# An empty place between the choice of experts and its counts, in a mixture of experts that runs between attention matmuls

## The chip, the cores and the metric

The kernel runs on one core of one Trainium2 chip. The metric is the device time of one execution in microseconds (us); the time before is the median of 3 runs. All data is fp32. A core has five engines that matter here, each with its own queue of instructions that it works off in order: TensorE (PE in the profile, its weight loads PEld), VectorE (DVE), ScalarE (ACT), GpSimd (POOL) and SyncE (SP, which here starts plain DMA transfers). Instructions wait for other engines through semaphores.

## The reference: what is computed

Four layers on x of 4 blocks by 512 tokens by 128 features. Each layer adds half a feed-forward part, an attention, and half a feed-forward part again, each after a layernorm:

```
x = x + 0.5 * ffn(layernorm(x));  x = x + attn(layernorm(x));  x = x + 0.5 * ffn(layernorm(x))
```

The change is in layer 2's feed-forward part, a mixture of 8 experts in which each token goes to one expert, and an expert takes at most 64 tokens of a block (n: 512 tokens, e: 8 experts, c: 64 slots):

```
gates = softmax(x @ Wg);  expert_idx = argmax(gates);  mask = one_hot(expert_idx)
gate = sum(gates * mask)
pos = cumsum(mask, axis=tokens) * mask - mask          # place in the expert's queue
keep = mask * (pos < 64)
dispatch = keep[..., None] * one_hot(pos, 64);  combine = dispatch * gate
expert_inputs  = einsum('bnd,bnec->becd', x, dispatch)
h              = gelu(einsum('becd,edh->bech', expert_inputs, W1))     # 512 hidden
expert_outputs = einsum('bech,ehd->becd', h, W2)
out            = einsum('becd,bnec->bnd', expert_outputs, combine)
```

Layer 2's attention is causal with 16 heads of 8, layer 3's the same without the mask. Layer 3's feed-forward part works on channels (a receptance gate, a squared ReLU, and a shift by one token).

## The kernel before, in words

**Where the time of interest lies.** Layer 2's attention of blocks 0 to 3 and layer 3's attention of blocks 0 to 3 are run as one list of 8 rows (`padded_attn_quick`). A row is worked off in 8 rounds. A round computes scores (L1462, PE, into `big`, a PSUM tile of 128 x 1024 of which there are three), the exponential (L1465, ACT, `pT`, six tiles), for causal rows a mask on the diagonal (L1469, DVE), and the values of the round before (L1475, PE, into `one`, a PSUM tile of 128 x 512 of which there are two). At the end of a row stand the sums by head (L1481, PE), a reciprocal (L1483, DVE), its spreading over the features (L1490, PE; L1492, DVE) and the output projection (L1497, PE; L326, DVE). At a row's beginning stand a layernorm, transposes (L315, PE), the products for values (L1435) and for keys and queries (L1444).

**What is put between.** Other work is written as Python generators whose pieces are fetched by `side` at three places of each round: A (L1599, ahead of the values), B (L1619, behind them) and C (L1622, behind the second half of the scores; `whole` is false there). `side` fetches up to three pieces at A and B and two at C. A piece tells by what it yields what the next one is: PE says that the next piece begins with matmuls, and then it is not begun at C; LATER says the same and also ends the place; WAIT only ends the place. A plan lists the streams with the first and the last row they may be in; `before(k)` works off what is due by row k. Layer 2 has four mixtures on two blocks each (two half layers, two pairs of blocks); the first half layer of blocks 0 and 1 is done by other code, and the other three (`l2_pair`) are in that plan. The first mixture (rounds 0 to 10) is the first half layer of blocks 2 and 3, the second (rounds 18 to 28) the second half layer of blocks 0 and 1, the third (rounds 34 to 44) the second half layer of blocks 2 and 3. After the second and the third, layer 3's channel streams follow in the plan (layernorm L295 on POOL, L304 on DVE; transposes L315; L1888, L1889 on DVE; L1894 on PE).

**The pieces of one mixture**, in the program's order: two layernorms; transposes and the router's products (L1640); softmax, the shares and the ranks of the experts (DVE); the choice `m` of the first expert (L1788, the trace calls it `chosen`) with its running sums (L1651, L1653) and the gates (L1644, L1645); then, after a LATER, the counts of tokens ahead of each token (L1658, L1659, PE), and the slots made of them (L1664 to L1675, L1798, L1799, DVE, `islot`); two empty places; eight scatters of normalised tokens into `pair_x` in HBM, two a piece (L1805, indirect DMAs on POOL); one load of all experts' inputs X, 512 KB (L1813, SP); three empty places; transposes of X (L1822, PE, one `big`) and their copy (L1823, DVE); four products with W1, each in a `big` of its own (L1830), copied to `hr` (L1832, DVE, 1.2 us each); gelu on the four (L1837, ACT, about 1.06 us each, another table of functions than the exponential's, so that a table load of 1.28 us stands at each change); two products with W2 (L1844), copied (L1846) and stored to HBM (L1847, SP, 256 KB each); two empty places; eight gathers by token (L1861, indirect DMAs on POOL, `yg`, four tiles), each token's result added to x with its gate (L1856, DVE, kept in the program's order).

**What sets the final order.** The generators and `side` set the order in which instructions are handed to the tile framework; its scheduler then sets each engine's own order by priorities and dependencies, so that an instruction can come out earlier or later than it was handed in. Some orders are fixed by hand: the adds L1856, the layernorm's outputs, and that the load of X waits for all eight scatters.

In the trace of before the first mixture's counts start at 906 us, its scatters run from 912.2 to 922.4, X's transposes start at 927.4 and the gathers at 960.1. In the second mixture the scatters start at 1045.5, X's transposes at 1064.7, the gathers at 1093.2; in the third the counts start at 1181.2, the scatters at 1188.0, the gathers at 1237.3.

Of the kernel before, what the change touches and what calls it, by code (L numbers as in the profile page):

```python
# [243 lines left out]
def program(ctx: ExitStack, tc: tile.TileContext, a: dict, out: bass.AP, worst):  # L244
# [12 lines left out]
    def one():  # L257
        return ps.tile([P, 512], F32, tag="one", name="one", bufs=2)
# [1372 lines left out]
    PE, LATER, WAIT = "PE", "PE later", "wait"  # L1631
# [10 lines left out]
    def l2_gates(sh, m, n, gt):  # L1642
        pick = tiny.tile([P, n, NE], F32, tag="pick", name="pick", bufs=1)
        nc.vector.scalar_tensor_tensor(pick, sh, 0.5, m, ALU.mult, ALU.mult)  # L1644
        nc.vector.tensor_reduce(gt, pick, AX.X, ALU.add)  # L1645

    def l2_sofar(m, n):

        v = m.rearrange("p (i t) e -> p i t e", i=n)
        sofar = tiny.tile([P, n, NT - 1, NE], F32, tag="sofar2", name="sofar2", bufs=1)  # L1650
        nc.vector.tensor_copy(sofar[:, :, 0, :], v[:, :, 0, :])  # L1651
        for t in range(1, NT - 1):
            nc.vector.tensor_tensor(sofar[:, :, t, :], sofar[:, :, t - 1, :], v[:, :, t, :], ALU.add)  # L1653
        return sofar
# [99 lines left out]
    def l2_pair(w, work, rows, rooms, key):  # L1754
# [33 lines left out]
        nc.vector.tensor_scalar(m, rank, 1.0, None, ALU.is_lt)  # L1788
        sofar = l2_sofar(m, 2)
        l2_gates(sh, m, n, gates)  # L1790
        yield LATER
        pp = one()
        before = pp[:, : n * NE].rearrange("p (t e) -> p t e", t=n)
# [236 lines left out]
    with tc.tile_pool(name="w13", bufs=1, reuse_waits="tile") as wp:  # L2030
# [50 lines left out]
        else:  # L2081
            deep[0] = 3
            rows = [(n, b, causal) for n, causal in (("l2", True), ("l3", False)) for b in range(B)]
            with tc.tile_pool(name="work", bufs=1, reuse_waits="tile") as work:

                def mixture(i, key):
                    return l2_pair(w2, work, (2 * i, 2 * i + 1), pair_rooms[i], key)
# [48 lines left out]
```

## Time and profile before

| what | before |
|---|---|
| median of 3 runs | 1448.82 us (1446.33 to 1449.94) |
| profiled execution | 1449.85 us |
| its span, first to last instruction | 1448.1 us |
| mean granted TensorE clock | 0.929 of full speed |
| PE busy | 1265.3 us, 87% of the span |
| DVE busy | 964.2 us, 67% |
| ACT busy | 647.2 us, 45% |
| POOL busy | 289.3 us, 20% |
| wait of L1658 for `chosen`, first two paired mixtures | 5.0 us, 2 waits |
| the same, third mixture | 0.7 us, 1 wait |

All times in the profile come from one execution, the profiled one, and start at its first instruction. The rows used below come from a few views. A row of the timeline gives start, length, engine, line, operation, output and inputs with their shapes, the number of instructions in the group, and in square brackets the idle time ahead of it with what ended it. [...] A row of the view of waits gives the waiting line, the engine and line that it waited for, and the total, the number and the longest of these waits. A row of the view of windows gives a stretch of the span, its length, the busy time of each engine with the number of its instructions, then the granted clock of TensorE (1.00 is full speed), the share of the DMA engines and GB/s.

### The profile page before, as it was taken

Reading aid. Unit: us, or ns where it says so; the run is one execution under the profiler, and the core shown is the slowest. Engines: PE = TensorE matmul, PEld = TensorE weight load, DVE = VectorE, ACT = ScalarE, POOL = GpSimd, SP = SyncE. Lnnn points to the kernel's source line nnn. Section 1 sums busy time; section 2 is a strip of 40 time slices with the busy share of each in tenths; the row PEclk is TensorE's granted clock in tenths of the full one; section 3 lists DMA queues with packets and bytes.
Section 4 is the critical chain, followed back from the end, with each engine's and each line's share of the span. In section 5 each row is a group of like instructions: output and inputs, shape, how many; then the busy total and the mean of one; then the engine's idle time right before and its main releaser. Section 6 shows DMA issues by size and latency. Waiting matters only on the chain.

```text
span 1448.1 us, 19903 instructions
## 1 busy us (share of the span) xinstructions
PE 1265.3 (87%) x6894; PEld 657.8 (45%) x6894; DVE 964.2 (67%) x2395; ACT 647.2 (45%) x925; POOL 289.3 (20%) x279
## 2 busy tenths in 40 slices
PE   6899899999899999899875597889887899899995
PEld 3455453344253435455544484453454345433333
DVE  4796677989888885967776547466655744365324
ACT  2435346636445362345543243335343446445560
POOL 3420420322103020202344113220112120210000
PEclk9999899999999999999987698799899989989996
DMA  7123121111111020122114000010001000100000
GB/s 274 38 72 107 49 70 61 66 52 53 69 45 73 30 71 8 37 59 61 30 46 170 0 1 1 30 30 1 6 25 30 1 8 23 29 1 12 4 8 11
DMA packets 60097, 63.78 MB, mean 44 GB/s; under 512 B 11089, under 2 KB 51282, under 8 KB 59346
## 3 DMA queue, kind: packets, MB, share of 16 engines
q1 hardware_dynamic: 54354, 50.86, 10.3%
q0 software_dynamic: 5632, 11.55, 2.6%
q8 instruction: 58, 0.95, 0.3%
q14 instruction: 53, 0.43, 0.1%
HBM read 28.95 MB, written 16.65 MB: 31 GB/s over the span
## 4 chain that ended last, share of the span: by engine, by line
PE 58%; DVE 20%; issue 11%; ACT 4%; POOL 3%; DMA 1%; SPq 1%; another core or an unknown queue 1%; POOLq 0%; DVEq 0%; ACTq 0%
PE big L1462 7%; PE big L734 7%; PE one L1475 6%; PE big L1043 5%; PE one L1057 5%; ACT pT L1465 2%; PE big L993 2%; PE one L767 2%; PE one L1497 2%; PE one L1086 2%; DVE sums L1052 2%; PE one L315 1%; PE big L1830 1%; PE one L1844 1%; PE big L1444 1%
## 5 line engine op out<-in xcount | busy, mean ns | idle before, releaser
L1465 ACT ACTIVATE pT<-big 128x1024 f32<-128x1024 f32 (+3 forms) x256 | 205.3, 866 | 235.1 <-PE big L1462 213.8
L1462 PE MATMUL big<-qkq,qkk 32*128 32x512 f32 (+3 forms) x1024 | 180.9, 581 | 30.7 <-ACT pT L1465 19.6
L734 PE MATMUL big<-w_w,xsT 128*128 x312 | 151.8, 610 | 0.4 <-issue 0.3
L1044 ACT ACTIVATE pT<-big 128x1024 f32<-128x1024 f32 x128 | 125.8, 1035 | 55.0 <-PE big L1043 52.4
L295 POOL TENSOR_TENSOR rs<-rs,root 128x4 f32<-128x4 f32 x51 | 56.8, 1116 | 422.9 <-DVE rs L294 368.2
L1043 PE MATMUL big<-qk 64*128 64x512 f32 x512 | 126.6, 605 | 6.8 <-DVE U L1079 6.8
L1475 PE MATMUL one<-pT,V 128*32 128x512 f32 (+3 forms) x1024 | 124.0, 570 | 1.3 <-DVE pT L1469 0.9
L1462 PEld LDWEIGHTS big<-qkq,qkk 32*128 32x128 f32 x1024 | 65.5, 193 | 119.7 <-ACT pT L1465 49.3
L815 POOL DMA_INDIRECT yg<-sorted_y,ito x64 | 72.1, 1126 | 225.6 <-DMA sorted_y<-ys 78.2
L1057 PE MATMUL one<-pT,V 128*64 128x512 f32 x512 | 116.9, 598 | 0.0
L559 POOL DMA_INDIRECT sorted_x<-xn,irows x64 | 70.5, 1102 | 70.3 <-DVE share L531 22.4
L1052 DVE TENSOR_TENSOR sums<-sums,pT 128x1024 f32<-128x1024 f32 x64 | 78.1, 1220 | 5.1 <-ACT qk L995 0.5
L1043 PEld LDWEIGHTS big<-qk 64*128 64x128 f32 x512 | 46.3, 186 | 69.0 <-issue 40.6
L1469 DVE TENSOR_TENSOR pT<-pT,w_c_tri 128x256 f32<-128x256 f32 x128 | 51.8, 421 | 38.7 <-ACT pT L1465 35.7
L734 PEld LDWEIGHTS big<-w_w,xsT 128*128 128x128 f32 x312 | 54.7, 196 | 41.4 <-issue 41.3
L1057 PEld LDWEIGHTS one<-pT,V 128*64 128x64 f32 x512 | 33.9, 136 | 77.1 <-issue 72.4
L1613 DVE COPY U<-one 128x512 f32<-128x512 f32 x32 | 22.0, 689 | 70.4 <-PE one L1475 54.5
L579 PE MATMUL big<-xnT,w_w 128*128 128x512 f32 x128 | 61.3, 616 | 6.6 <-DVE u L584 5.5
L1475 PEld LDWEIGHTS one<-pT,V 128*32 128x32 f32 x1024 | 29.8, 116 | 79.6 <-issue 61.6
L741 DVE TENSOR_TENSOR us<-big,t1s 128x1024 f32<-128x1024 f32 (+1 forms) x40 | 47.8, 1195 | 26.8 <-PE one L724 22.3
L1134 ACT COPY U<-one 128x512 f32<-128x512 f32 x32 | 18.8, 586 | 94.9 <-PE one L1057 87.8
L326 DVE TENSOR_TENSOR x<-x,one 128x512 f32<-128x512 f32 x31 | 21.2, 685 | 55.7 <-PE one L1086 17.9
(349 smaller groups left out, 2296.0 us busy)
## 6 DMA issues: line engine op xcount, KB each, us to landing
other<-qk SPq DMA_DIRECT2D x64, 256.0 KB
xs<-sorted_x SPq DMA_DIRECT2D x78, 64.0 KB
sorted_y<-ys SPq DMA_DIRECT2D x38, 128.0 KB
w_w<-in_w SPq DMA_DIRECT2D x2, 2048.0 KB
w_l_w<-in_l_w SPq DMA_DIRECT2D x2, 2048.0 KB
X<-pair_x SPq DMA_DIRECT2D x3, 512.0 KB
pair_y<-y SPq DMA_DIRECT2D x6, 256.0 KB
w_w<-in_w SPq DMA_DIRECT2D x1, 1152.0 KB
```

Source lines behind the costliest of these rows:

```text
L295: nc.gpsimd.tensor_tensor(rs, rs, root, ALU.pow)
L559: apart(nc.gpsimd.indirect_dma_start(out=sorted_x[:, :], out_offset=bass.IndirectOffsetOnAxis(ap=irows[:, b, j, t : t + 1], axis=0), in_=x ...
L579: nc.tensor.matmul(pa[:, m, :], lhsT=w["w13"][:, NE, m, odd, c * P : (c + 1) * P], rhs=xTs[b], start=True, stop=True)
L734: nc.tensor.matmul(pa[:, k, :], lhsT=st[u]["xT"][:, k * P : (k + 1) * P], rhs=w["w13"][:, bass.ds(st[u]["e"][k], 1), m].rearrange("p o a b ...
L815: nc.gpsimd.indirect_dma_start(out=y, out_offset=None, in_=sorted_y[: done(b) * P, :], in_offset=bass.IndirectOffsetOnAxis(ap=ito[:, b, j, ...
L1043: nc.tensor.matmul(sT[:, u, :], lhsT=k[r, t * P : (t + 1) * P], rhs=q[r, :], start=True, stop=True)
L1044: nc.scalar.activation(pT[:, :, t % 2, :], sT, AF.Exp, scale=scale)
L1052: nc.vector.tensor_tensor(s, s, pT[:, :, m, :], ALU.add)
L1057: nc.tensor.matmul(po[r, :], lhsT=V[:, t, :], rhs=pT[:, u, t % 2, :], start=(t == 0), stop=(t == NT - 1), tile_position=(0, 64 * u))
L1462: nc.tensor.matmul(sT[j // 2][:, j % 2, :n], lhsT=kT[r, t * P : (t + 1) * P], rhs=qT[r, S - n :], start=True, stop=True)
L1465: nc.scalar.activation(pT[j2][:, :, :n], sT[j2][:, :, :n], AF.Exp, scale=scale)
L1475: nc.tensor.matmul(po[32 * j : 32 * j + 32, S - n :], lhsT=V[k % 2][:, t, NJ * g + j, :], rhs=pT[j // 2][:, j % 2, :n], start=(t == 0), st ...
```

## The change

After the piece that chooses the experts and hands out the gates, one empty place is added. The piece with the counts begins with LATER as before. Lines behind it move by one: L1822 of before is L1823 after.

```diff
@@ -1788,6 +1788,7 @@
         nc.vector.tensor_scalar(m, rank, 1.0, None, ALU.is_lt)
         sofar = l2_sofar(m, 2)
         l2_gates(sh, m, n, gates)
+        yield WAIT
         yield LATER
         pp = one()
         before = pp[:, : n * NE].rearrange("p (t e) -> p t e", t=n)
```

`side`, which is not changed, reads what a piece yields:

```
for _ in range(3 if whole else 2):
    if not plan or plan[0][0] > k or (state.next in (PE, LATER) and not whole):
        return
    streams = plan[0][2]
    state.next = next(streams[0], streams)
    ...
    if state.next in (LATER, WAIT):
        return
```

No instruction is added to or taken from the mixture's arithmetic by the change; the pieces behind the empty place are handed in one place later each. All three mixtures have the added place.

## The prediction

> **What bounds the kernel now.** I read the page first: how busy each engine is, and the chain that ended last.
>
> ```profile
> PE 1265.3 (87%) x6894; PEld 657.8 (45%) x6894; DVE 964.2 (67%) x2395; ACT 647.2 (45%) x925; POOL 289.3 (20%) x279
> ...
> PE 58%; DVE 20%; issue 11%; ACT 4%; POOL 3%; DMA 1%; SPq 1%; another core or an unknown queue 1%; POOLq 0%; DVEq 0%; ACTq 0%
> ```
>
> PE is the bound where the change acts: attention matmuls fill it and layer 2's mixture is slotted between them. The change takes no work away, so it can only move PE's waits and its clock. PE's waits between 885 and 1115 us, where the first two paired mixtures run (releaser; us in total, times, longest), say how much there is:
>
> ```profile
> PE big L1462 <- ACT pT L1465: 13.4, 11, 4.5
> PE one L1658 <- DVE chosen L1788: 5.0, 2, 2.6
> PE one L315 <- DVE xns L304: 3.2, 3, 2.4
> PE big L1822 <- DMA X<-pair_x: 2.0, 1, 2.0
> ```
>
> The wait of L1658 for `chosen` is what an empty place ahead of the counts is aimed at. A gap also costs clock. Windows of 2 us (columns: window, length, busy us of PE, PEld, DVE, ACT, POOL, then the granted clock):
>
> ```profile
> 904.00:906.00 2.00, 0.00 (x0) 0.00 (x0) 2.00 (x5) 1.48 (x2) 0.00 (x0) 1.00 0.00 0
> 906.00:908.00 2.00, 1.76 (x6) 1.07 (x6) 1.29 (x10) 0.00 (x0) 0.00 (x0) 0.63 0.00 0
> 908.00:910.00 2.00, 2.00 (x12) 1.58 (x12) 0.73 (x4) 0.00 (x0) 0.00 (x0) 0.50 0.00 0
> ...
> 914.00:916.00 2.00, 2.00 (x20) 0.67 (x20) 0.88 (x3) 1.80 (x4) 1.68 (x2) 1.00 0.09 35
> ...
> 932.00:934.00 2.00, 2.00 (x12) 1.22 (x8) 0.31 (x1) 1.37 (x2) 0.00 (x0) 0.54 0.01 4
> 934.00:936.00 2.00, 2.00 (x20) 2.00 (x19) 0.89 (x3) 1.98 (x3) 0.00 (x0) 1.00 0.00 0
> ```
>
> After PE's 2.37 us gap the clock falls to 0.50 at 906.5 and is 1.00 again before 914. I take from the rows: a gap of 2.04 us or more costs some 6.3 us of half clock, that is 3.1 us of work, and one up to 1.48 us costs none (1224 to 1226 us stands at 1.00 after such a gap).
>
> [...] This trace shows the fall after 2.37 us, and I go by the trace.
>
> **What the change does.** One WAIT more makes `side` return once more, so every later piece of a mixture comes one place later. No instruction is added by the program. The compiled order of each engine, after against before, tells what that moves. SP's and POOL's orders stay, with the X load, the y stores, the 8 scatters and 8 gathers in their old succession: nothing is moved past anything on those queues. PE's, DVE's and ACT's change.
>
> *The counts.* In mixtures 1 and 2 they keep their place in PE's order. The 5.0 us of waits for `chosen` therefore stay, and so does the half clock behind them: gain 0. Only in mixture 3 do they move, behind eight value matmuls (L1475) instead of one.
>
> *Mixture 1.* PE met the X transposes before X had landed:
>
> ```profile
> 920.95 1.22 PE L1462 MATMUL big<-qkq,qkk 32*128 32x256 f32 x4 [3.36 <-ACT pT L1465]
> 922.11 3.21 PE L1475 MATMUL one<-pT,V 128*32 128x512 f32 x16
> ```
>
> After that came a gap of 2.04 us ended by X's DMA. Now eight score matmuls (about 0.5 + 2 us at full clock) and L315's stand ahead of L1822, ready: -2.0 us. The clock fell at 920.3 and came back at 933, since the second gap broke the recovery; uninterrupted it would be back after 6.3 us, at about 926.8. Of the 6.2 us up to 933, 2.0 were the gap, 4.2 work at half speed: -2.0, of which I take -1.9. Against it stand the gelus, now in two groups (three, then one), with score exps between. The third `hr` copy (1.22), the third gelu (1.06), a table load (1.28) and the exp of a 384 pair (0.80) follow the third product: 4.36 us, under which PE has scores (0.9 + 0.6), four value matmuls (0.95) and one L1844 (0.23), 2.7 in all: a wait of 1.7. The two next tiles, behind the last gelu's loads, I put at 0.8. Together 2.5 where 1.66 us is idle now (0.46 + 1.20): +0.8. Sum **-3.1**; bounds -1.2 (the clock does not recover) and -5.6 (the new waits vanish).
>
> The table loads are the price of splitting. ACT in mixture 3, where before already splits:
>
> ```profile
> 1224.04 1.02 ACT L1465 ACTIVATE pT<-big 128x1024 f32<-128x1024 f32 x1
> 1225.08 1.28 ACT L1837 ACT_TABLE_LOAD   x1
> 1226.38 1.06 ACT L1837 ACTIVATE hr<-hr 128x1024 f32<-128x1024 f32 x1
> 1227.45 1.28 ACT L1465 ACT_TABLE_LOAD   x1
> 1228.74 2.86 ACT L1465 ACTIVATE pT<-big 128x1024 f32<-128x1024 f32 x3
> ```
>
> A load starts where the last exp ends and the next exp starts 1.30 us after the load did. The order has 16 loads around gelu and exp instead of 8: 8 x 1.30 = 10.4 us more on ACT, hidden by its 55% of idle time except in the waits counted here; without that cover all 10.4 would be lost. [...]
>
> *Mixture 2.* The reciprocal L1483 now stands ahead of the `hr` copies:
>
> ```profile
> 1219.65 3.36 DVE L1483 RECIPROCAL rsum<-one 128x512 f32<-128x512 f32 x1 [1.14 <-PE one L1481]
> ```
>
> So the first `big` comes free 3.36 us later; along the rows that makes waits of 1.0 and 0.7 us where 0.97 and 1.10 are now: -0.4. y is stored and the first gather starts some 3.9 us later (now 1093.20). The sixth gather already waits 3.90 us for an add (L1856, held by 4 `yg` buffers), so this is just covered; uncovered it costs up to 3.9. On DVE the four adds of the second block no longer stand ahead of L304; they and their neighbours put L304 at 1110.42 although POOL's rs was done at 1108.47. So of the wait at L315,
>
> ```profile
> 1110.81 1.24 PE L315 MATMUL one<-w_c_ident,xns 128*128 128x128 f32 x4 [2.37 <-DVE xns L304]
> ```
>
> 1.3 us go. Sum **-1.7**; bounds -4.4 (all named waits go) and +3.9.
>
> *Mixture 3.* Before, PE's order and its gap:
>
> ```profile
> 1178.60 1.92 PE L1475 MATMUL one<-pT,V 128*32 128x512 f32 x2
> 1181.24 0.60 PE L1658 MATMUL one<-chosen,w_c_before 128*128 128x32 f32 x2 [0.73 <-DVE chosen L1788]
> ```
>
> The 0.73 goes, and the clock, at 0.50 from 1176.5 to 1185.7, can be back after 6.3 us, at 1182.8: 2.9 us at half speed, -1.5. Then the reciprocal stands ahead of `hr` here too: counting PE's products (1.85 a quad) and scores against DVE's 3.36 + 1.22 + 0.8 + 2 x 1.22 and ACT's loads, PE waits 0.1 + 0.15 + 1.15 + 0.6 = 2.0 us instead of 1.48: +0.5, and one load more may show: +1.8; I take +1.2. The gathers come about 4 us later; from rs (1248.43) to L315 (1257.22) there are 8.8 us, of which mixture 2 needed 3.4, so 5.4 are free and cover it. Sum **-1.0**; bounds -3.7 and +1.6 (+1.8 for the load, 2.0 for gathers over the slack, less 2.2).
>
> **Total:** -3.1 - 1.7 - 1.0 = -5.8 from the profiled execution's 1449.85 (span 1448.1), 1444.05; it stands 1.03 above the median 1448.82, so **1443 us** on the median. The bounds add up to -13.7 and +4.3.
>
> **Rivals.** (1) *It doesn't do what it says:* the counts stay put in two of three mixtures, the clock in mixture 1 does not recover (-1.2), and what mixture 3 gains (-2.2) goes to the late `hr` copies and loads (+2.5). -1 us: 1448. For it: two unchanged counts. Against: the X wait of 2.04, whose place PE fills with ready work. (2) *Slower: three `big` buffers held by late `hr` copies.* The new waits of 1.2 to 1.7 us lie just under the gaps that cost clock. If each is some 0.6 us longer, all pass 2.04 and each mixture pays 3.1 more: -5.8 + 3 x (3.1 + 0.6) = +5.3, 1454. It decides between 1.48 and 2.04 us of gap. For it: split gelus, reciprocal first. Against: before has such gaps at 1.48 without a fall. (3) *The 4.5 us wait for pT in mixture 2 goes.* It ends an ACT stall during the scatters, whose releaser the trace does not name; I leave it. If the shift dissolves it, 4.5 and 3.1 of clock go: 1436.
>
> **How the numbers follow.** Forecast 0.46 (1438 to 1447), rival (1) 0.26 (1445 to 1451), (2) 0.23 (1451 to 1460), (3) 0.05. A measurement tells about 0.3%, 4.3 us, from no change: faster is below 1444.5, slower above 1453.2. Faster: 0.37 of the forecast, all of (3) and 0.02 of (1): 0.44. Slower: 0.18 of (2) and 0.02 of others: 0.20. Same: 0.36. The range 1436 to 1455 goes from the lower bound to a little above the upper one.
>
> **What would show it.** Right: the X wait of L1822 gone, clock 1.00 from about 927 us in mixture 1; waits for `chosen` still twice over 2 us; 16 table loads; L315's long wait near 1 us; the last gathers in mixture 3 done over 3.4 us before L315. Wrong: half clock beginning at the W1 products or the scores behind them (rival 2), gathers that L315 waits for, or new unnamed ACT stalls during the scatters.

## The result, and the profile after

The change made the kernel slower: the median of 20 runs is 1456.16 us, that of 20 runs of before 1449.01 us; the ratio is 1.0044, 95% interval 1.003 to 1.0058, some 6.4 us. (One run of 2381 us is left out of the ratio.) The profiled execution took 1453.55 us, its span is 1451.8 us, the mean granted clock 0.932.

The page of after, the same two rows as in the prediction:

```profile
PE 1262.5 (87%) x6894; PEld 654.7 (45%) x6894; DVE 963.9 (66%) x2395; ACT 657.0 (45%) x933; POOL 289.9 (20%) x279
...
PE 62%; DVE 21%; issue 7%; ACT 5%; POOL 3%; another core or an unknown queue 1%; DMA 1%; POOLq 0%; SPq 0%; DVEq 0%; ACTq 0%
```

PE does the same work. ACT has 933 instructions instead of 925 and 9.8 us more busy time: the eight table loads that the order of the engines had told. Now PE's waits from 885 to 1115 us:

```profile
PE one L1658 <- DVE chosen L1788: 6.0, 2, 3.5
PE big L1895 <- issue: 3.7, 1, 3.7
...
PE one L315 <- DVE xns L304: 0.8, 2, 0.6
```

The wait for X is gone; the waits for `chosen` are still there twice; L315 hardly waits, but L1895 (the first channel product, L1894 of before, where it waited 2.96 us) does.

To see where the two traces part, I count the score instructions (L1462 on PE, 1024 in each trace, from 1 in order of start; a product of the program stands as two instructions on PE in these traces, the eight of a W1 tile as x16, and a transpose of X as one, L1822 x8) and compare when the same one starts. The difference after minus before is -1.9 us at the first one (ahead of all that the change touches), -7.5 at the 305th (behind mixture 1), -1.7 at the 513th (behind mixture 2), +4.9 at the 801st (behind mixture 3) and +3.7 at the end. So in this pair of profiles mixture 1 gained 5.6 us, mixture 2 lost 5.8 and mixture 3 lost 6.6. The first two of these are mostly half clock. Its cost, half of PE's busy time at half clock (a group of 16 value instructions, L1475 on 128x512, took 3.64 us at 0.50 and 1.92 at 1.00 in after), is 13.9 us in before and 6.1 in after up to the 305th score instruction, and 14.7 and 21.1 from there to the 513th; PE's idle time differs by under 0.6 us in either part. A single pair of profiles can't say how much of that is the change. But each experiment leaves some mixtures alone, so that its trace is one more sample of before's or of the change's order in a stretch. These are the lengths of some stretches in all 16 traces (us; from one score instruction to another; "old" and "new" are before's order and the change's order in that stretch):

| stretch | old order | new order |
|---|---|---|
| mixture 1, 33rd to 281st | 112.4 to 113.2 (7 traces) | 108.5 to 112.3 (9) |
| mixture 2, 449th to 465th: idle time of PE in it | 5.28 to 5.40 (7) | 6.77 to 7.17 (9) |
| mixture 3, 577th to 609th: the counts | 16.8 to 17.1 (7) | 17.94 to 17.95 (5), 12.7 to 13.7 (4) |
| mixture 3, 609th to 705th: the products | 59.0 to 59.3 (5) | 64.8 to 65.7 (5) |

The products' row holds the traces of before's products and of the change's products without another edit there; the other six are told with their experiments. This row is where the loss shows. Within each order it hardly varies, and the orders are 5.5 us or more apart.

The traces are of two kinds, and this bears on the first two rows. In before, after and e9 to e12, where before takes 1449 to 1450 us, ACT has stalls of 2.0 to 6.8 us in mixture 1 or 2 whose releaser the profile does not name. In the other ten traces there is none; on their chips before takes 1438 to 1441 us. There PE waits 6.4 to 6.5 us for X in mixture 1 in the old order and still 3.7 to 5.1 us in the new one, so that "the wait for X is gone" holds for after, e9, e11 and e12 only. What the stalls are stays open. The row of the products does not depend on the kind.

### The profile page after: what moved, and what is told of

It is laid out like the page before. It is cut to its first block, busy times and chain, and to the rows that moved or that the text cites. A ratio compares the mean times of both kernels' runs of the same rounds, so it can differ in the third digit from the quotient of the medians.

```text
span 1451.8 us, 19919 instructions
## 1 busy us (share of the span) xinstructions
PE 1262.5 (87%) x6894; PEld 654.7 (45%) x6894; DVE 963.9 (66%) x2395; ACT 657.0 (45%) x933; POOL 289.9 (20%) x279
## 4 chain that ended last, share of the span: by engine, by line
PE 62%; DVE 21%; issue 7%; ACT 5%; POOL 3%; another core or an unknown queue 1%; DMA 1%; POOLq 0%; SPq 0%; DVEq 0%; ACTq 0%
PE big L1462 8%; PE big L734 6%; PE one L1475 6%; PE big L1043 6%; PE one L1057 6%; ACT pT L1465 3%; PE one L1086 2%; PE big L993 2%; PE one L1845 2%; PE one L1497 2%; PE big L1831 2%; PE one L767 1%; POOL rs L295 1%; PE one L315 1%; DVE st L291 1%
## 5 line engine op out<-in xcount | busy, mean ns | idle before, releaser
L1462 PE MATMUL big<-qkq,qkk 32*128 32x512 f32 (+3 forms) x1024 | 182.9, 586 | 33.1 <-ACT pT L1465 23.2
L1475 PE MATMUL one<-pT,V 128*32 128x512 f32 (+3 forms) x1024 | 125.3, 575 | 1.9 <-DVE pT L1469 0.9
L1462 PEld LDWEIGHTS big<-qkq,qkk 32*128 32x128 f32 x1024 | 65.9, 195 | 121.8 <-ACT pT L1465 53.1
L1475 PEld LDWEIGHTS one<-pT,V 128*32 128x32 f32 x1024 | 29.6, 116 | 80.7 <-issue 61.5
```

The costliest lines, as they stand in the source:

```text
L1462: nc.tensor.matmul(sT[j // 2][:, j % 2, :n], lhsT=kT[r, t * P : (t + 1) * P], rhs=qT[r, S - n :], start=True, stop=True)
L1475: nc.tensor.matmul(po[32 * j : 32 * j + 32, S - n :], lhsT=V[k % 2][:, t, NJ * g + j, :], rhs=pT[j // 2][:, j % 2, :n], start=(t == 0), st ...
```

## The experiments

Each group of runs had its own runs of before on the same chip beside it (medians 1438.2 us for e1 to e4, 1440.6 for e5 to e8, 1449.6 for e9 to e12, 1439.6 for e13 and e14), so ratios are compared, not times. Differences in us are the ratio times the group's median of before. The change itself was not run again in these groups. The trace of a run is one execution of ten or twelve, whose times spread over 7 to 15 us.

### Which mixture, and which part of it

**e1, e2, e3: the empty place in one mixture alone.** The edit, with slots2 and slots3 for the other two:

```diff
-        yield WAIT
+        if key == "slots1":
+            yield WAIT
         yield LATER
```

> The empty place in the first paired mixture alone; the orders of the engines differ from before only in that stretch. Theory A (the loss comes in mixtures 2 and 3, the first one gains as forecast): 1 to 5 us faster than before, about 1446. Theory B (each place costs alike, because a split group of gelus costs ACT loads everywhere): 2 us slower, about 1451. Theory C (no stretch is to blame, the clock's fall at random moments makes the difference): within 1 us of before.

> The empty place in the second paired mixture alone. Theory A: 2 to 6 us slower than before (the two profiles lie 5.8 us further apart behind this stretch than ahead of it), about 1453. Theory B: 2 us slower. Theory C: within 1 us of before. The forecast's own step would have it 1.7 us faster.

> The empty place in the third paired mixture alone. Theory A: 4 to 7 us slower than before (the two profiles lie 6.6 us further apart behind it), about 1454; PE waits over 1 us for an exponential behind a table load that comes after the last gelu. Theory B: 2 us slower. Theory C: within 1 us. The forecast's own step would have it 1.0 us faster.

Measured: 1.0009 (0.9989 to 1.0028), 1.0011 (0.9988 to 1.0033) and 1.0025 (1.0005 to 1.0046): +1.3, +1.6 and +3.6 us. Only the third differs from no change by its interval. Theory A's numbers were missed all three times, in e2 and e3 narrowly. The forecast's own -3.1 for mixture 1 and -1.0 for mixture 3 lie outside the intervals of e1 (-1.6 to +4.0 us) and e3 (+0.7 to +6.6). By the times alone theory B (2 us each) isn't excluded. The stretches of the table do not bear it out: in e3's trace the products of mixture 3 take 64.8 us, in e1's and e2's 59.0.

**e4: the empty place behind the counts.**

```diff
-        yield WAIT
         yield LATER
...
         nc.vector.tensor_copy(islot, slot)
         yield WAIT
         yield WAIT
+        yield WAIT
```

> The empty place stands behind the counts instead of ahead of them, in all three mixtures: everything from the scatters on is one place later, as in the change, but the counts of mixture 3 stand where before has them. If the later pieces carry the loss: as slow as the change, 5 to 8 us over before. If moving the counts carries it (the half clock in mixture 3 lasted 17 us in the profile after, 10 us before): no more than 3 us over before. The forecast's step for the counts (2.2 us gained) would have it 2 us slower than the change.

Measured 1.0038 (1.0021 to 1.0056), +5.5 us: nearly the whole loss without moving the counts.

**e14: mixture 3's products alone.** One place more behind the load of X, for the third mixture:

```diff
-        for _ in range(3):
+        for _ in range(4 if key == "slots3" else 3):
             yield WAIT
```

> Before, with one empty place more behind the load of X in mixture 3 alone: only its products, gelus and gathers come later; counts, scatters and mixtures 1 and 2 stand as in before. If these later products carry the whole loss: 4 to 7 us slower than before, and the stretch from the 609th to the 705th score instruction takes 64 to 65.5 us instead of 59.0. If the counts' place were needed for the loss: within 2 us of before.

Measured 1.0038 (1.0019 to 1.0057), +5.5 us, and 65.18 us in the stretch. Mixture 3's later products alone make a loss of nearly the change's size; both expected numbers came.

**e12: mixtures 1 and 2 alone** (the place unless the key is slots3).

> The empty place in mixtures 1 and 2 alone. If mixture 3 alone carries the loss, and the first one gains 2.9 us as the lengths of its stretch say (112.7 us in three profiles of before's order, 109.9 in three of the change's): 1 to 4 us faster than before. If each mixture costs a little: 2 to 4 us slower than before.

Measured 0.9995 (0.9976 to 1.0014): no change that can be told. The expected 1 to 4 us did not come: mixture 1's stretch took 108.5 us, 4.6 less than in e10 of the same group (113.1, before's order), but mixture 2 gave some of it back (below), and the rest is inside the interval.

### What the later products of mixture 3 run into

e14 has nothing else in it, so I read it there. PE's rows:

```profile
1190.56 1.14 PE L1462 MATMUL big<-qkq,qkk 32*128 32x512 f32 x8
1192.49 1.50 PE L1462 MATMUL big<-qkq,qkk 32*128 32x512 f32 x8 [0.79 <-DVE qkq L1450]
1193.93 1.09 PE L1822 MATMUL big<-w_c_ident,X 128*128 128x128 f32 x8
1194.95 1.92 PE L1475 MATMUL one<-pT,V 128*32 128x512 f32 x16
...
1204.22 3.04 PE L1462 MATMUL big<-qkq,qkk 32*128 32x512 f32 x12
1208.42 1.65 PE L1462 MATMUL big<-qkq,qkk 32*128 32x512 f32 x4 [1.17 <-ACT pT L1465]
...
1228.15 1.13 PE L1462 MATMUL big<-qkq,qkk 32*128 32x512 f32 x4 [1.59 <-ACT pT L1465]
```

Four waits: 0.79 us for qkq; some 1.05 hidden in the group at 1204.22 (3.04 us, where twelve take 1.99 in e6, below), for a `hr` copy behind the reciprocal; 1.17 for the exps; 1.59 for the exps again. The same work in before:

```profile
1205.89 1.09 PE L1822 MATMUL big<-w_c_ident,X 128*128 128x128 f32 x8
1206.91 3.44 PE L1462 MATMUL big<-qkq,qkk 32*128 32x512 f32 x16
1210.28 5.62 PE L1830 MATMUL big<-XT,w_l_w 128*128 128x128 f32 x48
...
1224.14 2.10 PE L1462 MATMUL big<-qkq,qkk 32*128 32x512 f32 x8 [1.48 <-DVE hr L1832]
...
1237.82 2.27 PE L1462 MATMUL big<-qkq,qkk 32*128 32x512 f32 x12 [0.47 <-DVE U L1492]
```

The wait for qkq is no new cost. The sixteen scores and the X transposes take 4.39 us from their first start to the next row in both kernels (1190.56 to 1194.95, and 1205.89 to 1210.28); in before the waiting is hidden in the group of sixteen. ACT's rows of e14 tell the last two waits:

```profile
1207.34 2.86 ACT L1465 ACTIVATE pT<-big 128x1024 f32<-128x1024 f32 x3
...
1216.21 1.06 ACT L1837 ACTIVATE hr<-hr 128x1024 f32<-128x1024 f32 x1
1225.78 1.28 ACT L1465 ACT_TABLE_LOAD   x1 [8.51 <-PE big L1462]
1227.08 3.77 ACT L1465 ACTIVATE pT<-big 128x1024 f32<-128x1024 f32 x4
```

The load at 1225.78 is the thing to see: ACT is idle for 8.51 us after the last gelu, and yet the load of the exponential's table does not start until the scores that the exponential waits for are there. It goes in front of the exps at full length, and the next scores wait for free `big` tiles. Then the clock, by windows of e14:

```profile
1206.00:1208.00 2.00, 1.25 (x6) 0.30 (x4) 0.07 (x1) 1.97 (x3) 0.00 (x0) 1.00 0.00 0
1208.00:1210.00 2.00, 1.58 (x5) 0.30 (x5) 0.00 (x0) 2.00 (x3) 0.00 (x0) 0.72 0.00 0
1210.00:1212.00 2.00, 2.00 (x11) 2.00 (x10) 0.00 (x0) 1.97 (x3) 0.00 (x0) 0.50 0.04 8
```

The clock goes to half behind the thin stretch of scores, and a second time behind the 1.59 us wait: 6.83 us of busy time at half clock, none in before. Over the stretch PE is idle for 4.53 us where before has 2.99, so +1.54; half clock costs 6.83 / 2 = +3.41; the rest of PE's busy time, in which waits inside groups are hidden, grows from 56.09 to 57.24, +1.15. Together this is the 6.10 us by which the stretch is longer (65.18 against 59.08). The shares are e14's: in the trace of after the stretch has only one window of half clock (+1.71) and more idle time (+2.73), a wait of 1.03 us without a named releaser among it, and is 5.74 us longer.

**e5: the table fetched at once.**

```diff
             nc.scalar.activation(h, h, AF.Gelu_apprx_tanh)
+        tiny = work.tile([P, 1], F32, tag="tiny", name="tiny")
+        nc.scalar.activation(tiny, hs[-1][:, 0, :1], AF.Exp)
         yield LATER
```

> The change, with an exponential of one column (128 x 1, its result unused) behind the last gelu of each mixture, so that ACT fetches the exponential's table at once and not when the next scores are there. Theory L (in mixture 3 the table load that stands behind the last gelu, and waits with the scores, is what makes PE wait 1.59 us): that wait falls to some 0.4 us, and the clock does not fall behind it; 1.2 to 3 us faster than the change, so 3 to 5 us over before. Theory R (the late copies of hr behind the reciprocal carry the loss): as slow as the change, 5.5 to 7 us over before.

Measured 0.9972 (0.9957 to 0.9987): 4 us faster than before, not 3 to 5 slower. The wait did fall:

```profile
1226.99 1.13 PE L1462 MATMUL big<-qkq,qkk 32*128 32x512 f32 x4 [0.26 <-ACT pT L1465]
```

But the stretch only went to 63.46 us: the other waits and half clock behind the first scores (6.30 us) stayed. So the wait's cause is shown; that this alone is worth 10 us between the change's ratio and e5's is not, and neither theory's time came. In e5's trace the counts' stretch of mixture 3, ahead of the wait that was removed, took 13.5 us instead of 17.9 (see the clock, below).

**e6: the reciprocal behind the copies of hr**, for the two rows concerned:

```diff
-                        step(ends[0])
+                        if k1 not in (2, 4):
+                            step(ends[0])
...
             side(ended, True)
+            if r and h1 and g1 == NG - 1 and k1 in (2, 4):
+                step(ends[0])
```

> The change, with the row's end (sums by head and reciprocal) of rows 2 and 4 handed in behind the place with the first three W1 products instead of ahead of it; on DVE three copies of hr then stand ahead of the reciprocal again in mixtures 2 and 3. Theory R: the waits of the scores behind these copies in mixture 3 (1.17 us shown and some 1.0 us between matmuls of one group) shrink to what before had, 0.7 to 2.5 us faster than the change, so 4 to 5.5 us over before. Theory L: within 0.5 us of the change.

Measured 0.9988 (0.9969 to 1.0008). The hidden wait went (the group of twelve takes 1.99 us again), and the one behind it grew:

```profile
1199.97 1.99 PE L1462 MATMUL big<-qkq,qkk 32*128 32x512 f32 x12
1203.79 1.13 PE L1462 MATMUL big<-qkq,qkk 32*128 32x512 f32 x4 [1.83 <-ACT pT L1465]
```

Three gelus now stand ahead of the exps instead of two. The stretch is 63.90 us, 0.9 under the change's 64.82. The late copies are worth at most about that here; theory R in its strong form falls. The whole time again moved by more than the stretch, and neither theory's time came. So the products' stretch does not set the whole time alone: in e5 and e6 it is still 4.4 and 4.9 us longer than in e8 of the same group (59.02), and yet they are not slower than before. In their traces the counts' stretch is 3.2 to 3.4 us shorter than in e8's.

**e7: one gelu over all four tiles.**

```diff
+        hr = work.tile([P, NE // 2, 2, NH * P], F32, tag="hr", name="hr", bufs=1)
...
-            h = work.tile([P, 2, NH * P], F32, tag="hr", name="hr", bufs=NE // 2)
+            h = hr[:, q]
...
-        for h in hs:
-            nc.scalar.activation(h, h, AF.Gelu_apprx_tanh)
+        nc.scalar.activation(hr, hr, AF.Gelu_apprx_tanh)
```

> The change, with the four hr tiles in one tile and one gelu over 128 x 4096 in place of four: no exponential can come between, and ACT has 6 table loads less around the gelus than before, 10 less than the change (39 in the program instead of 41 and 49). If splitting the gelus is what costs: at most 2 us over before. If not: the scores wait for one block of 3.5 us instead, 6 us over before or more.

Measured 0.9985 (0.9964 to 1.0005): the loss is gone. (The trace has 19 table loads where before has 21 and after 29, so 2 and 10 less; the expectation's 6 is wrong.) In mixture 3 the four exps now run ahead of the one gelu, no score waits more than 0.4 us for an exp, and only W2 waits for the gelu:

```profile
1203.17 3.44 PE L1462 MATMUL big<-qkq,qkk 32*128 32x512 f32 x16
...
1213.56 3.84 PE L1845 MATMUL one<-w_l_w,hr 128*128 128x128 f32 x32 [1.20 <-ACT hr L1838]
```

The stretch takes 59.42 us with no half clock in it, though the products come as late as in the change and the third copy of `hr` comes as late (it ends 7.30 us after the reciprocal starts, here and in e14). So with the exps out of their way, late products and late copies cost some 0.4 us there; what costs is that gelus and table loads stand ahead of exps that the next scores wait for. It is not the split by itself: before splits these gelus too (three, then one) and takes 59.1 us.

**e8: before with the tiny exponential.** The edit of e5 on before.

> Before, with the same exponential of one column behind the last gelu of each mixture. Theory L: before's loads stand mostly under work, so 0 to 1 us faster than before. If the exposed loads cost more than the profile of before shows: 2 us faster or more.

Measured 0.9988 (0.9969 to 1.0006), 1.7 us faster, not told from none; the products' stretch stays at 59.02 us.

### The counts, and the clock's grid

**e10: the counts alone moved.** The place ahead of the counts, and one less behind the load of X:

```diff
-        for _ in range(3):
+        for _ in range(2):
             yield WAIT
```

> The empty place ahead of the counts, and one empty place less behind the load of X: the counts alone are moved (in mixture 3, behind eight value matmuls), products, gelus and gathers stand where before has them. If the counts are to blame for the change's loss: 3 us or more over before. If the later products are: within 1.5 us of before, and faster by up to 3 us if theory P holds and the clock comes back early there; the stretch from the X transposes on in mixture 3 takes 59.0 us as in before.

Measured 0.9976 (0.9959 to 0.9993), 3.5 us faster than before, a little more than expected, with 59.21 us in the products' stretch. The counts' stretch takes 13.70 us, 3 less than in before; in the change's trace, with the same order of PE there, it takes 17.95 us, 1 more. The windows of e10, then of after, behind the counts:

```profile
1184.00:1186.00 2.00, 2.00 (x20) 1.71 (x18) 1.13 (x3) 0.00 (x0) 0.00 (x0) 0.78 0.00 0
1186.00:1188.00 2.00, 1.67 (x14) 0.61 (x8) 0.85 (x6) 1.34 (x2) 0.69 (x1) 1.00 0.00 0
```

```profile
1186.00:1188.00 2.00, 2.00 (x8) 0.20 (x8) 0.00 (x0) 1.59 (x3) 1.39 (x3) 0.50 0.08 33
1190.00:1192.00 2.00, 2.00 (x12) 0.74 (x10) 0.00 (x0) 0.00 (x0) 1.39 (x3) 0.53 0.15 61
```

In e10 the clock is back within 1184 to 1186, after 6.83 us at half; in after it stays at half for 17.07 us although PE has no gap at all. What differs is when the fall begins. Counted from the 577th score instruction, it begins 0.32 to 0.49 us later in all five traces that take 17.9 us, and earlier in the others: 0.14 and 0.05 us later than that instruction in e10 and e6, 0.49 ahead of it in e5 (13.5 to 13.7 us), and none at all in e7 (12.70). With the counts in their old place, the six falls that begin 0.14 to 0.75 us later all last 10.24 us; the seventh, in e2, begins 4.30 us later and lasts 6.83.

**e9: four transposes done twice** ahead of these counts, to shift the program against the clock:

```diff
+            if key == "slots3" and b == rows[0]:
+                transposed(xn)
             nc.scalar.copy(xnT, transposed(xn))
```

> The change, with four transposes of mixture 3's first block done twice (L315; the second result is unused): 0.6 us more work for PE shortly ahead of the counts of mixture 3. Theory P (how long the clock stays at half ahead of and behind these counts hangs on where the 3.41 us grid of the clock's changes falls in the program, not on where the counts stand): the stretch from the 577th to the 609th score instruction, which holds the counts, takes 13 to 14.5 us instead of 17.95, though it is preceded by more work, and the whole is 0 to 4 us faster than the change, so 2 to 6 us over before. Rival (moving the counts lengthens the half clock by itself): that stretch stays at 17.9 us or more and the whole is 0.6 us slower than the change.

Measured 1.0048 (1.0028 to 1.0069), and 17.95 us: theory P's number did not come, and the rival's did (17.9 us or more, and 7.0 us over before where the change has 6.4). But the experiment did not do what it was for: the stretch with the extra transposes, from the 545th to the 577th score instruction, took 18.19 us with them and without them, so PE's extra work was hidden there and the fall still began at 0.32 us. In nine traces the length goes with the moment of the fall; that the moment is the cause, and that it can be moved at will, was not shown.

**e11 and e13: what helped, put together.** e11 is the change with mixture 3's products in their old place and the tiny exponential; e13 is e10 with the tiny exponential. Their edits are those of e5 and e10 (in e11, the shorter loop for slots3 only).

> Put together from what helped: the empty place in all three mixtures, in mixture 3 one empty place less behind the load of X (its products stay where before has them), and the exponential of one column behind the last gelu. If the loss is mixture 3's later products with their split gelus: 4 us faster than e5 at most, 5 to 8 us under before. If not: no faster than e5, 4 us under before.

> The counts alone moved (as e10) and the exponential of one column behind the last gelu of each mixture. If the gain of e10 (3.5 us) and that of the early table load are each real and independent: 4 to 6 us faster than before. If the load's gain shows only where the gelus are split by the change (e8 left it open, 1.7 us with an interval across zero): as e10, 2.5 to 4 us faster.

Measured 0.9995 (0.9973 to 1.0016) and 0.9992 (0.9973 to 1.001): neither can be told from before, and all the expected gains failed. Both have 17.9 us in the counts' stretch, and 61.2 and 60.6 us in the products' (one window of 3.41 us at half clock each). The waits of PE in that stretch are before's own (1.48 and some 0.47 us), but the half clock isn't. e5 and e10 are the versions that beat before by their intervals, each measured once. e13, which holds e10's order, does not; its trace shows where (the counts' stretch), but not why.

## Why the prediction was wrong

It foretold 1443 us (gain 5.8); measured is a loss of 6.4. The step that failed is the one on the products of mixture 3, put at +1.2 with nothing for the clock; they cost +5.7 to +6.5. The gains of mixtures 1 and 2, -4.8 together, did not show in the whole time either: e12 measured -0.7 us (-3.5 to +2.0). By its steps:

- **Orders.** SP, POOL, the unmoved counts of mixtures 1 and 2 (6.0 us, twice) and 16 loads were as read.
- **The clock's price.** Half clock was read as some 6.3 us behind each gap from 2.04 us up. The falls come in steps of 3.41 us: the one at 906.5 lasted 6.83, the one at 1176.2 lasted 10.24 and came with no gap of PE ahead of it.
- **Mixture 1, -3.1: the mechanism was right in the traces of the result's kind, the size partly by luck.** Its stretch is 4.5 us shorter in after, e9, e11 and e12 (108.5 to 108.7) than in before and e10 (113.2 and 113.1), and 0.1 to 2.9 us shorter in the others, where X's wait is shorter but not gone. In after X's wait is gone, and the clock, which falls at 918.8 us, is back at 922.2 (foretold 926.8; 933.8 in before):

```profile
922.00:924.00 2.00, 2.00 (x18) 0.82 (x16) 1.15 (x3) 1.08 (x3) 0.00 (x0) 0.95 0.89 239
924.00:926.00 2.00, 2.00 (x22) 1.46 (x24) 0.88 (x3) 1.99 (x3) 0.00 (x0) 1.00 0.10 28
```

  So half clock gave 4.4 us instead of 1.9, the idle time only 1.1 instead of 2.0 (the wait for `chosen` grew from 2.37 to 3.51), and the rest of PE's busy time grew by 1.0.
- **Mixture 2, -1.7: failed.** Of the wait at L315 1.3 us were to go. In the change's own profile this wait does go, from 2.37 to 0.6 us, but two others take its place. PE in before; PE, then ACT, in after:

```profile
1115.01 2.05 PE L1894 MATMUL big<-t,w_l3f_wk 128*128 128x512 f32 x2 [2.96 <-issue]
```

```profile
1103.19 2.08 PE L1462 MATMUL big<-qkq,qkk 32*128 32x512 f32 x4 [3.10 <-ACT pT L1465]
...
1113.04 2.04 PE L1895 MATMUL big<-t,w_l3f_wk 128*128 128x512 f32 x2 [3.70 <-issue]
```

```profile
1102.75 1.57 ACT L1465 ACTIVATE pT<-big 128x256 f32<-128x256 f32 x3 [4.66 <-remote]
```

  The first of the two in after comes from an ACT stall without a named releaser ("remote") during the gathers. It stands in after, e9, e11 and e12 and not in before and e10, so such stalls (rival 3) are there in both orders, but in these six traces this one comes with the new order. In e2 and e4 to e7 there is no stall; there L315 still waits 2.1 to 2.4 us, and the product behind it 4.7 to 4.8. PE, then DVE, in e2:

```profile
1092.33 1.24 PE L315 MATMUL one<-w_c_ident,xns 128*128 128x128 f32 x4 [2.14 <-DVE xns L304]
1098.25 2.04 PE L1896 MATMUL big<-t,w_l3f_wk 128*128 128x512 f32 x2 [4.68 <-issue]
```

```profile
1094.23 0.61 DVE L1858 SCALAR_TENSOR_TENSOR x<-yg,gate,x 128x128 f32<-128x128 f32 x2
...
1095.43 0.61 DVE L1858 SCALAR_TENSOR_TENSOR x<-yg,gate,x 128x128 f32<-128x128 f32 x2
1095.95 0.88 DVE L1890 TENSOR_SCALAR t<-xnT,nmu 128x511 f32<-128x511 f32 x2
```

  The four adds of the second block did leave their place ahead of the normalised tokens, but they went behind them, ahead of the channel part's `t`, and PE's next product waits for that. (The PE row names no releaser; that `t` is it follows from the product's input.) Either way PE's idle time there is 6.8 to 7.2 us in all nine traces of the new order, where before has 2.37 + 2.96 = 5.33: +1.4 or more instead of -1.3. I had not asked what is late next. The products ahead of it (353rd to 417th score instruction) take 0.7 to 5.8 us less than the old order in the same group (e7, whose order differs there, left out), and half clock around L315 takes that back in some traces: 9.3 to 9.8 us of it in after, e9, e11 and e12, 3.0 to 4.9 in the other five, 3.7 to 3.9 in the old order. The 5.8 us that mixture 2 lost in the pair of profiles are half clock (above), for which the forecast had nothing; e12, with the same order, has 16.5 us of that cost where after has 21.1.
- **Mixture 3, the counts, -2.2: not to be had at will.** The stretch is 3 us shorter in e10 and 1 us longer in the change's profile, with the same order.
- **Mixture 3, the products, +1.2: this is the step that sank the forecast.** Measured +5.7 to +6.5. It foresaw the late `hr` copies and "one load more". Its waits, 2.0 us and 0.7 more for that load, are 1.05 + 1.17 + 1.59 = 3.81 us in e14, the last of them the load's; and it put the clock at nothing, since no wait seemed to pass 2.04 us, where e14 has 3.41 us.
- **Rival (2)** (1454 us, chance 0.23) has the time that came, in one mixture instead of three, and by scores that wait for late exps more than for late `hr` copies. Its point of decision was wrong: in e14 the clock fell behind waits of 1.05 + 1.17 close together, and behind one of 1.59; in after, with the same waits, it fell behind the one of 1.59 alone. The gathers came 4.8 us later in mixture 3 and were covered, as foretold (the eighth at 1251.8, L315 at 1262.4).

e14's +5.5 us, e12's -0.7 and the counts' stretch of the change's profile, +1.2, add up to 6.0 of the 6.4; they are from different chips, so this is an estimate.

## What to carry to other kernels

When a piece is moved by one place, ask at each wait that is to go what is late next. Compare whole stretches and not only named waits: a wait that a view names after the change can have stood before it, hidden in a group. Keep calls of one function table together where another engine's tiles hang on the same queue, or make them one instruction; in e14 the 1.28 us table load behind the last gelu started only 8.51 us after it, when the scores of the next exps were there, and stood in front of these exps. And where a stage's clock falls after thin stretches, a sum of waits alone can be off by as much again: in e14 half clock cost 3.41 us beside 3.81 us of waits. To price waits of 1.05 and 1.17 us close together with a window of half clock is an estimate from e14; after has the same two waits and no fall behind them. Before a stretch of one profile is explained by the change, look whether the traces of other chips have it too.

## What the runs showed of the hardware

In these runs the granted clock changed on a grid. In all 16 traces every stretch at half clock lasts 1 to 5 times 3.41 us (413 stretches; the one that the end of each trace cuts off is not counted), and within a trace all changes lie on one grid of 3.41 us, whose position differs from run to run. The clock fell behind a wait of 1.59 us in e14 and in after (at 1243.1 us there), and after none at all where PE ran the router's products (128 x 8 outputs, L1639) beside scores for one window, as ahead of the fall at 1176.2 us in before.

PE was busy and the clock still fell, or stayed at half: PE was 100% busy in that window of before, and in the 17.07 us of half clock in after. In e14 a window of 3.41 us with 8 score instructions was 66% busy and was followed by half clock; in before a window that was 62% busy with 8 score instructions and 7 instructions of W1 products was not. What sets off a fall was not tried.

In these runs a gain in one place stood beside new half clock in another. In e11 and e13 PE idles 3.45 and 2.93 us in the products' stretch, about as in before (2.99), yet one window of half clock stands there that before has not, and the stretch is 2.1 and 1.6 us longer. That the earlier change brings it is not shown.
